# A two-layer spectral-convolution attention kernel: order of the work written out unit by unit, with five regroupings of its products

## The chip, the cores and the metric

The kernel runs on one core of one Trainium2 chip. The metric is the device time of one execution in microseconds (us); lower is better. Engines: PE (TensorE, matmuls), PEld (its weight loads), DVE (VectorE), ACT (ScalarE), POOL (GpSimd), SP (SyncE, which issues most transfers).

## The reference, cut to what matters

The input x has 2 batches of 56 planes of 128 x 128 points, all float32. Two layers of the same form follow each other, each `x = x + layer(gn(x))`:

```python
def layer(x, ...):                      # B, K, H, W = 2, 56, 128, 128; A = 8 heads
    xa = x.reshape(B * K, 1, H, W)
    xn = inorm(xa, g1, b1)
    k, q, v = (fno_layer(xn, ...) for each)          # 1 -> 8 channels
    scores = einsum('baks,bals->bakl', qh, kh) / sqrt(H * W)
    out = einsum('bakl,bals->baks', softmax(scores), vh)
    out = fno_layer(out, Pw, Pb, Psw, Psb)           # 8 -> 1 channel
    att = inorm(out + xa, gan, ban)
    an = inorm(att, g2, b2)
    h = fno_layer(an, M0..., norm=True, act=True)    # gelu
    h = fno_layer(h, M1..., norm=True)
    return inorm(h, gmo, bmo) + att

def fno_layer(x, w, b, sw, sb, norm=False, act=False):
    y = spectral_conv(x, w, b)          # rfft2, 2 x 16 x 16 modes times complex weights, irfft2
    if norm: y = inorm(y)
    y = y + skip1x1(x, sw, sb)
    return gelu(y) if act else y
```

`gn` normalises groups of 4 of the 128 positions of the last axis.

## The kernel before, in words

Everything is one function, `fno_layers` (L167). X2 holds x in SBUF, two halves of rows on partitions 0 to 55 and 64 to 119. P (8192 columns per batch) first holds the turned planes, later scratch and the gelu's output. WU, WT and WM hold block-diagonal mode weights; when these are done their room serves FB and `half`. Matmul results go to two PSUM pools: `bank` (2 buffers of one bank) and `pair` (3 buffers of two).

For each layer and each of the two batches the steps are:

- `turned` (L352) transposes X2 to planes by PE, ACT copies them to P, DVE takes `bn_stats` (L371).
- `modes_chain` (L457) gets mean and deviation, scales the planes (L479 on DVE, L477 on ACT, in four parts), transforms each part along one axis by PE (L483), turns it by DVE (L488), transforms along the other (`to_modes`, L384), and makes `gvr`, a row of 1/deviation for every position (L501).
- `gram` (L506, 128 products into one bank) and `gram_chain` give variances per plane.
- `scores` (L566): for each of four steps, 32 small products U x (L597, 64x64 weights from WU times 56 columns of modes) into a pair. The tile position is `(64 * e, 64 * e)`, so two of the array's four quarters are in use. ACT copies the pair (L602), and products with the modes add up the scores (L578).
- `scale_x` (L547) multiplies X2 by `gvr` on DVE, eight instructions a batch (L550), and sends the row to partitions 56 and 120.
- `values`, `softmax_chain`, `mix_chain`, `heads`, `norms_chain` (L611 to L746). `rows_of` (L427) makes diagonal matrices on DVE (L432) and `spread` (L435) turns them into rows on all partitions by one product with ones.
- `gelu` (L787): inverse transform by PE (`synthesis`, L753), skip product from X2 (`mixed`, L768), Gelu on ACT (L835), statistics (L837), turning back (L817), forward transform (L805).
- `h_chain` (L846): the modes of h, its weights, norms, `inverse`.
- `end` (L903): `synthesis` and `mixed` again, DVE adds the scaled h (L943). Then, in layer 0 and for batch 0 of layer 1, POOL adds the raw x (L946), which `moved` (L909) has loaded into one of three `xr` buffers, from the input x in layer 0 and from the DRAM buffer `store` in layer 1. In layer 0 the sum is the new X2, batch 0 is also written to `store`, and `turned` makes the next planes. For batch 1 of layer 1 (`last`), DVE divides X2 by the scale instead (L775) and PE adds it into the same pair (`add_x`, L782).

`prepare` (L237, on POOL) makes the mode weights of a layer compact; `relay` (L310) exchanges their axes in three groups, each one transpose, four DVE products with a mask and eight products on PE (L327); `build` (L334) and `build_m` spread them into WU, WT, WM on POOL (L337, L345).

The order of the work: every step is a generator that yields an estimated cost. `_woven` (L141) runs one step's units and fills each with units of another until the cost is reached; lines 961 to 1003 say which steps are woven. Instructions may then still be moved by the scheduler, which sorts each engine's instructions by priority and readiness; only those under `keep_in_program_order` stay put. A float32 matmul stands as two instructions in the trace, a transpose as one.

Of the kernel before, what the change touches and what calls it, by code (L numbers as in the profile page):

```python
# [57 lines left out]
def _constants():  # L58
# [26 lines left out]
    for r in range(2):  # L85
# [26 lines left out]
        "m16": (p[:, None] // 8 == np.arange(16)) * 1.0,  # L112
# [28 lines left out]
def _woven(lead, *bulks):  # L141

    rest = chain(*bulks)
    for want in lead:
        while want > 0:
            cost = next(rest, None)
            if cost is None:
                break
            yield cost
            want -= cost  # L150
    yield from rest


def _with(bulk, extra):

    for cost in bulk:
        next(extra, None)
        yield cost


def _run(units):
    for _ in units:
        pass
# [3 lines left out]
def fno_layers(ctx: ExitStack, tc: tile.TileContext, x, out, weights, small, const):  # L167
    nc = tc.nc
    V, S, G, T = nc.vector, nc.scalar, nc.gpsimd, nc.tensor
# [7 lines left out]
    dp = pool("dram", 1, space=bass.MemoryType.DRAM)  # L177
# [14 lines left out]


    Ct = cp.tile([N, N_CONST], F32, name="C")
    C = {k: Ct[:, o : o + n] for k, (o, n) in _PARTS.items()}
    ident = C["ident"]
    nc.scalar.dma_start(out=ident, in_=const["all"][:, :N])
# [4 lines left out]
    for b in range(B):  # L202
        for g in range(0, 8, 2):
            for c in range(2):
                nc.sync.dma_start(
# [3 lines left out]
            if (b, g) == (0, 4):  # L209
                nc.sync.dma_start(out=Ct[:, N:], in_=const["all"][:, N:N_CONST])  # L210
        if b == 0:
            for n in range(2):
                nc.sync.dma_start(out=smt[n], in_=small[n : n + 1, :].to_broadcast([N, N_SMALL]))
            nc.sync.dma_start(out=stage[:, :1088], in_=weights[0].rearrange("p m r n t -> p (m r n t)"))
    for b in range(B):
        nc.sync.dma_start(out=X2[K:64, b], in_=x[b, :8, :64, :])
    eps = cp.tile([N, 1], F32, name="eps")
    V.memset(eps, EPS)
    ones = cp.tile([N, N], F32, name="ones")
# [14 lines left out]
    store = dp.tile([1, K, N, N], F32, name="store")  # L234


    def prepare(layer):  # L237
        sml = smt[layer]
# [31 lines left out]
        tt(col("m2"), par["m1sw"], par["m1sw"], ALU.add)  # L270
        tt(Wf, Wf, _bc(rawc[:, 0], 1, 2 * N_W), ALU.mult)
        tt(M, M, _bc(rawc[:, 1:3], 2, N_W), ALU.mult)
        tt(W, W, M, ALU.add)
        tt(W[:, 0, 0:32, :], W[:, 0, 0:32, :], _bc(sml[:, 0:32], 2, 8), ALU.add)
        t64 = [stage[:, 544 + 64 * n : 608 + 64 * n].rearrange("p (a t) -> p a t", a=8) for n in range(4)]
# [29 lines left out]
        product(0, 1, 0, True, ss, g2, 3)  # L305
        product(16, 3, 2, False, vp, par["g1"], 5)
        place(cpt[:, 32:36].rearrange("p (n c) t -> p n c t", c=2), W[:, 0, 32:34, :], W[:, 1, 32:34, :], 5)
        return par, d, cpt, little(f"tc{layer}", [N, 8, 36])

    def relay(cpt, tcs, room, groups):  # L310

        L = room.rearrange("p (t e c j s) -> p t e c j s", t=8, e=2, c=2, j=4)
        for o, n in groups:
            rows = 8 * n
            pa = bank()
            T.transpose(pa[:rows, :N], cpt[:, o : o + n, :].rearrange("p n t -> p (n t)"), ident)
            src = pa[:rows, :N].rearrange("p (j c e t) -> p j c e t", j=4, c=2, e=2)
            for e in range(2):
                for c in range(2):
                    V.tensor_tensor(  # L320
# [363 lines left out]
    def heads(L, b, st):  # L684
# [3 lines left out]
        for t in range(8):  # L688
# [6 lines left out]
            if t % 2:  # L695
                yield 1.0
# [358 lines left out]
```

## Time and profile before

| what | us |
|---|---|
| median of 3 timed runs | 552.59 |
| the 3 runs | 560.3, 551.16, 552.59 |
| profiled execution, its own time | 547.76 |
| span of the profiled execution, first to last instruction | 546.0 |
| mean granted PE clock in it, as a share of full speed | 0.919 |

The profile is one execution. Busy times are of one engine each and overlap each other. A wait named in brackets is the idle time of an engine ahead of an instruction, with the one that ended it.

### The profile page before, as it was taken

The numbers are of one execution on the slowest core, as the hardware profiler recorded it, in microseconds if no ns is written. First come the engines' busy times: TensorE is split into PE (matmuls) and PEld (weight loads), VectorE is DVE, ScalarE is ACT, GpSimd is POOL, SyncE is SP. The second block draws the span as 40 slices with busy tenths as digits, with TensorE's granted clock in tenths as the row PEclk, the third lists the DMA queues.
The fourth block names the chain that finished last, engine by engine and source line by source line (L and its number), as shares of the span: only waits on it lengthen the run. The fifth ranks groups of instructions, "written<-read, shape, count | busy, mean of one in ns | idle before, by whom it ended". The sixth has DMA issues, their size and how long they took to land.

```text
span 546.0 us, 14842 instructions
## 1 busy us (share of the span) xinstructions
PE 458.8 (84%) x6696; PEld 315.0 (58%) x6696; DVE 318.6 (58%) x556; ACT 190.3 (35%) x242; POOL 158.5 (29%) x205
## 2 busy tenths in 40 slices
PE   2467999898699999989587799989599999986695
PEld 2325869686485566636443468778376556544431
DVE  1465352926735784777578562717715775766585
ACT  2443330524435436614223240344237356502000
POOL 2297509950000000044539924000000000055300
PEclk9998898989797998989679999999797998988698
DMA  8994001030100000016553320000000000027444
GB/s 181 232 196 73 4 2 46 4 89 2 20 2 2 1 2 1 1 35 212 175 136 100 98 78 6 3 4 4 2 3 1 1 2 1 1 56 236 149 129 141
DMA packets 13167, 33.24 MB, mean 61 GB/s; under 512 B 2080, under 2 KB 2848, under 8 KB 13088
## 3 DMA queue, kind: packets, MB, share of 16 engines
q1 hardware_dynamic: 12960, 32.23, 22.8%
q8 instruction: 52, 0.85, 0.7%
q10 hardware_dynamic: 144, 0.07, 0.1%
q14 instruction: 11, 0.09, 0.1%
HBM read 21.02 MB, written 11.01 MB: 59 GB/s over the span
## 4 chain that ended last, share of the span: by engine, by line
PE 53%; DVE 20%; POOL 7%; DMA 7%; ACT 6%; issue 5%; SPq 1%; DVEq 0%; POOLq 0%; ACTq 0%
PE pair L768 8%; PE pair L753 6%; PE pair L817 5%; POOL X L946 5%; PE pair L597 5%; PE bank L511 5%; PE bank L691 3%; DMA X<-x 3%; PE bank L805 3%; DMA xr<-x 3%; DVE WT L404 2%; DVE X L550 2%; PE bank L578 2%; PE bank L442 2%; PE bank L327 2%
## 5 line engine op out<-in xcount | busy, mean ns | idle before, releaser
L371 DVE BATCH_NORM_STATS2 stats<-P 128x6 f32<-128x448 f32 x64 | 36.1, 614 | 48.2 <-ACT P L366 32.3
L837 DVE BATCH_NORM_STATS2 stats<-P 128x6 f32<-128x512 f32 x64 | 40.7, 678 | 20.3 <-ACT P L835 20.3
L943 DVE SCALAR_TENSOR_TENSOR P<-P,hs,pair 128x1024 f32<-128x1024 f32 x32 | 40.1, 1270 | 12.7 <-PE pair L768 12.5
L835 ACT ACTIVATE P<-pair 128x1024 f32<-128x1024 f32 x32 | 32.6, 1025 | 32.4 <-PE pair L768 31.8
L946 POOL TENSOR_TENSOR X<-P,xr 128x1024 f32<-128x1024 f32 x16 | 37.5, 2355 | 19.4 <-DMA xr<-x 11.2
L393 POOL MEMSET WT<- 128x256 f32 x4 | 1.3, 313 | 139.4 <-PE bank L805 92.9
L817 PEld LDWEIGHTS pair<-C,P 120*128 120x128 f32 x256 | 29.0, 152 | 21.2 <-issue 8.5
L550 DVE TENSOR_TENSOR X<-X,gvr 120x1024 f32<-120x1024 f32 x32 | 40.3, 1303 | 0.0
L768 PE MATMUL pair<-X,Bs 57*64 57x512 f32 x256 | 40.2, 671 | 0.0
L768 PE MATMUL pair<-X,Be 57*64 57x512 f32 x256 | 38.6, 705 | 0.0
L817 PE MATMUL pair<-C,P 120*128 120x120 f32 x256 | 36.8, 291 | 0.5 <-DVE P L404 0.5
L511 PE MATMUL bank<-P 128*64 128x56 f32 (+1 forms) x1024 | 37.2, 238 | 0.0
L511 PEld LDWEIGHTS bank<-P 128*64 128x64 f32 (+1 forms) x1024 | 35.5, 152 | 2.1 <-issue 1.5
L597 PEld LDWEIGHTS pair<-xf,WU 64*64 64x64 f32 x1024 | 32.8, 135 | 5.3 <-issue 4.5
L597 PE MATMUL pair<-xf,WU 64*64 64x56 f32 x1024 | 35.9, 221 | 0.0
L818 ACT COPY WT<-pair 128x896 f32<-128x896 f32 x32 | 28.9, 906 | 14.0 <-PE pair L817 12.5
L753 PE MATMUL pair<-C,WT 32*128 32x128 f32 x512 | 24.1, 294 | 9.1 <-DVE WT L404 4.4
L753 PEld LDWEIGHTS pair<-C,WT 32*128 32x128 f32 x512 | 19.4, 189 | 20.5 <-issue 12.0
L369 ACT COPY P<-pair 128x896 f32<-128x896 f32 x16 | 14.5, 907 | 46.3 <-PE pair L363 46.3
L361 PE MATMUL pair<-C,X 56*128 56x56 f32 x256 | 16.7, 282 | 16.4 <-DMA X<-x 10.7
L363 PE MATMUL pair<-C,X 120*128 120x120 f32 x128 | 18.8, 297 | 13.4 <-POOL X L946 13.4
L363 PEld LDWEIGHTS pair<-C,X 120*128 120x128 f32 x128 | 14.9, 155 | 23.3 <-POOL X L946 20.0
(235 smaller groups left out, 850.0 us busy)
## 6 DMA issues: line engine op xcount, KB each, us to landing
X<-x SPq DMA_DIRECT2D x16, 448.0 KB
xr<-x SPq DMA_DIRECT2D x32, 224.0 KB
out<-P SPq DMA_DIRECT2D x32, 224.0 KB
store<-X SPq DMA_DIRECT2D x16, 224.0 KB
xr<-store SPq DMA_DIRECT2D x16, 224.0 KB
stage<-weights SPq DMA_DIRECT2D x2, 544.0 KB
C<-const_all SPq DMA_DIRECT2D x1, 621.0 KB
X<-x SPq DMA_DIRECT2D x2, 256.0 KB
```

The source lines that it names most:

```text
L363: T.transpose(p[:, s, N * e : N * e + 120], X2[:120, b, i, :], ident[:120, :120])
L371: V.bn_stats(stats[:, 2 * g + s, :], dst[:, 448 * s : 448 * s + 448])
L511: T.matmul(p[u : u + m, :K], lhsT=P[b][:, K * i : K * i + m], rhs=plane[b][:, i, :], start=(i < 2), stop=(i == N - 1), tile_position=(0, u ...
L550: tc.keep_in_program_order(V.tensor_tensor(v, v, _bc(st["gvr"][:120], 1, 8), ALU.mult))
L597: T.matmul(p[64 * e : 64 * e + 64, k, K * a : K * a + K], lhsT=WUv[64 * e : 64 * e + 64, t + k, a, :], rhs=xv[64 * e : 64 * e + 64, t + k, ...
L753: T.matmul(both[j // 2][:, j % 2, N * e : N * e + N], lhsT=Z[32 * j : 32 * j + 32, o : o + N], rhs=C["gw"][32 * j : 32 * j + 32, :], start ...
L768: T.matmul(p[64 * c : 64 * c + 64, r, :], lhsT=Bs[q, :], rhs=X2[q, b, s : s + 4, :].rearrange("p e w -> p (e w)"), start=False, stop=stop, ...
L817: T.transpose(p[:, r, N * e : N * e + 120], h3[:120, o : o + N], ident[:120, :120])
L835: S.activation(h3, both[v].rearrange("p r m -> p (r m)"), AF.Gelu)
L837: V.bn_stats(stats[:, 4 * A + 2 * v + r, :], h3[:, 512 * r : 512 * r + 512])
L943: V.scalar_tensor_tensor(h3, h3, st["hs"], both[v].rearrange("p r m -> p (r m)"), ALU.mult, ALU.add)
L946: G.tensor_tensor(dst, h3, xr[:, n % 3, :], ALU.add)
```

## The change

- **Order.** `_woven`, `_with`, `_run` and the costs go. Each step is a stream of units named by a letter and 2 x layer + batch; `ORDER` lists 714 units, and each entry runs the stream to its next `yield`. At the end `_in_order` ties every instruction of DVE, ACT, POOL, PE and SP to the one before it on its engine, so that no scheduler moves them.
- **U x** is a stream of its own (`u_x`), its tile position runs through all four quarters, and the scores take one copy of the modes with its halves exchanged (`xs`, two ACT copies).
- **Factor rows.** `rows` multiplies a broadcast column with diagonal matrices that `diagonals` (POOL) made once a layer.
- **Relay.** One group: POOL (in layer 0 POOL and DVE) masks the compact weights, and eight products of 288 columns add up in one bank.
- **Norm scale in the transform.** The scale is multiplied into the transform's 32 columns (`fwg`), the shift is added to the modes; `normalise` scales the planes for the Gram product apart from that. Two parts share one DVE turn.
- `scale_x` moves from DVE to POOL. In layer 1 both batches divide X2 by the scale, on POOL into `xr` (`end_x`), and PE adds it; `store` and its transfers go. The constants of both layers come in one transfer.

```diff
+ORDER = """
+t0 t0 t0 t0 t0 W0 t0 k0 k0 k0 k0 k0 t0 t0 k0 k0 k0 m0 m0 m0 W0 m0 m0 n0 n0 n0 t1 t1 t1 t1 m0 k1 k1 k1 t1 t1 m0 m0 W0
+W0 t1 t1 W0 R0 R0 n0 n0 n0 R0 R0 R0 B0 k1 k1 g0 g0 k1 k1 g0 g0 g0 k1 g0 m1 B0 m1 g0 g0 A0 c0 m1 m1 C0 n1 n1 u0 u0 m1
...
+y1 h0 y1 y1 z1 z1 z1 b1 b1 h0 h0 f1 f1 b1 b1 f1 h0 f1 f1 f1 b1 h0 h0 b1 f1 h0 f1 f1 h1 h1 e0 e0 o0 e0 e0 o0 h1 h1 x0
+x0 x0 e0 o0 x0 e0 o0 x0 t2 k2 A1 h1 h1 e0 h1 e0 o0 e0 o0 h1 h1 x0 e0 e0 o0 x1 t2 h1 e0 o0 h1 h1 h1 k2 t2 k2 A1 A1 A1
+t2 t2 k2 x1 k2 e1 e1 e1 x1 t2 t2 o1 o1 t2 x1 e1 e1 e1 k2 k2 o1 o1 e1 k2 e1 e1 x1 o1 x1 m2 x1 x1 e1 o1 e1 o1 e1 m2 t3
...
+e3 x3 e3 e3 o3 e3 x3 o3 o3 o3 e3 o3
+"""
...
+def _in_order(tc, engines):
+
+    last = {}
+    for i in list(tc.nc.cur_bb.bb.instructions):
+        if i.engine in engines:
+            if i.engine in last:
+                info = mybir.DependencyInfo(mybir.DependencyClass.NoSync, mybir.DependencyReason.DATA)
+                tc.add_manual_dep(i, last[i.engine], info, reason="in order")
+            last[i.engine] = i.name
...
-                nc.sync.dma_start(out=Ct[:, N:], in_=const["all"][:, N:N_CONST])
+                Q.dma_start(out=Ct[:, N:], in_=const["all"][:, N:])
...
+    def relay(layer):
...
+            E.tensor_tensor(
+                r.rearrange("p (s t n) -> p s t n", s=n, t=8),
+                _bc(cpt[:, :, s0 : s0 + n].rearrange("p n s -> p s n"), 2, 8), _bc(_bc(C["m8"], 1, n), 3, 36), ALU.mult,
+            )
...
+                T.matmul(
+                    p[:, :288], lhsT=C["sel"][:, 7 - s : 7 - s + N], rhs=r[:, 288 * (s - s0) : 288 * (s - s0) + 288],
+                    start=(s == 0), stop=(s == 7), skip_group_check=True,
+                )
...
+    def rows(cols, of):
+
+        p = bank()
+        for n, (u, m) in enumerate(zip(cols, of)):
+            T.matmul(p[:, K * n : K * n + K], lhsT=u.to_broadcast([K, N]), rhs=m, start=True, stop=True)
...
+        fwg = little(f"fwg{b}", [N, 32])
+        S.activation(fwg, C["fw"], AF.Copy, scale=gv)
...
+        p = to_modes(mid, by_h[L][0])
+        V.tensor_tensor(grid(xf[:, :448]), grid(p), _bc(sx, 2, K), ALU.add)
...
-            tc.keep_in_program_order(V.tensor_tensor(v, v, _bc(st["gvr"][:120], 1, 8), ALU.mult))
+            G.tensor_tensor(v, v, _bc(gvr[:120], 1, 8), ALU.mult)
...
+    def u_x(L, b):
+
+        R = room(b)
+        xv = grid(st[L][b]["xf"][:, :448])
+        for t in range(0, 8, 2):
+            p = pair()
+            for k in range(2):
+                for a in range(4):
+                    for c in range(2):
+                        for e in range(2):
+                            o, n = 64 * (e ^ c), 224 * k + K * a
+                            T.matmul(
+                                p[o : o + 64, c, n : n + K], lhsT=WUv[64 * e : 64 * e + 64, t + k, 4 * c + a, :],
+                                rhs=xv[64 * e : 64 * e + 64, t + k, :], start=True, stop=True,
+                                tile_position=(64 * e, o), skip_group_check=True,
+                            )
...
+    def end_x(L, b):
...
+                G.tensor_tensor(
+                    xr[:120, n % 3, :].rearrange("p (c s w) -> p c s w", c=2, s=4),
+                    x8.rearrange("p (c v s) w -> p v c s w", c=2, v=2)[:, n % 2], _bc(_bc(inv[:120], 1, 4), 1, 2), ALU.mult,
+                )
...
+    for name in ORDER.split():
+        _step(tc, name, streams[name])
+    assert all(next(s, "end") == "end" for s in streams.values())
+    _in_order(tc, [e.engine for e in (V, S, G, T, Q)])
```

The letters of the order: t transposes, k their statistics, m modes, n scaling of the planes, g Gram product, c its chain, q scale of X, u U x, s scores, v values, a softmax and mix, d heads, p norms, y gelu, z its statistics, b turning back, f forward transform, h the h chain, x load or division of X, e sums of the end, o its output; W `prepare`, R relay, O diagonals, A, B, C the builds of WU, WT, WM.

## Rows read from the trace of the kernel before

**Rows 1.** The page: busy us, share and instructions; chain that ended last.
```profile
PE 458.8 (84%) x6696; PEld 315.0 (58%) x6696; DVE 318.6 (58%) x556; ACT 190.3 (35%) x242; POOL 158.5 (29%) x205
...
PE 53%; DVE 20%; POOL 7%; DMA 7%; ACT 6%; issue 5%; SPq 1%; DVEq 0%; POOLq 0%; ACTq 0%
```

**Rows 2.** Windows: stretch, length, busy us per engine, clock, DMA share, GB/s.
```profile
0.00:52.00 52.00, 26.75 (x287) 17.89 (x289) 22.75 (x49) 18.97 (x22) 27.78 (x84) 1.00 0.83 179
52.00:232.00 180.00, 167.25 (x2655) 125.95 (x2659) 102.96 (x202) 73.04 (x95) 45.92 (x65) 0.92 0.06 13
232.00:331.00 99.00, 79.77 (x1005) 47.81 (x1006) 66.26 (x100) 28.72 (x35) 55.52 (x35) 0.90 0.41 115
331.00:480.00 149.00, 138.30 (x2252) 100.50 (x2252) 84.25 (x161) 65.72 (x83) 10.48 (x13) 0.94 0.03 3
480.00:546.00 66.00, 46.77 (x512) 22.81 (x512) 42.37 (x48) 3.89 (x8) 18.76 (x8) 0.85 0.48 147
...
500.00:520.00 20.00, 11.26 (x86) 6.22 (x84) 12.16 (x22) 1.00 (x4) 7.88 (x4) 0.66 0.54 164
```

**Rows 3.** Timeline of PE, five bursts: start us, length us, line, operation, tiles, count.
```profile
345.04 2.08 PE L597 MATMUL pair<-xf,WU 64*64 64x56 f32 x64
...
393.17 1.09 PE L620 MATMUL pair<-WT,xf 64*64 64x256 f32 x16
...
78.87 1.96 PE L327 MATMUL bank<-C,stage 128*128 128x16 f32 x16
...
519.47 1.09 PE L782 MATMUL pair<-X,C 56*64 56x512 f32 x8
...
246.44 1.04 PE L363 MATMUL pair<-C,X 120*128 120x120 f32 x8
```

**Rows 4.** Groups by line and shape: count, busy us, mean ns, idle before.
```profile
L550 DVE TENSOR_TENSOR X<-X,gvr 120x1024 f32<-120x1024 f32 x32 | 40.3, 1303 | 0.0
...
L946 POOL TENSOR_TENSOR X<-P,xr 128x1024 f32<-128x1024 f32 x16 | 37.5, 2355 | 19.4 <-DMA xr<-x 11.2 <-DVE P L943 8.1
...
L337 POOL TENSOR_TENSOR WU<-tc,C 128x1024 f32<-128x1024 f32 x8 | 16.3, 2055 | 2.5 <-ACT tc L331 2.5
...
L479 DVE TENSOR_SCALAR P<-P,gv,sh 128x1792 f32<-128x1792 f32 x8 | 10.2, 1281 | 0.3
...
L775 DVE TENSOR_TENSOR X<-X,gvr 120x1024 f32<-120x1024 f32 x8 | 9.5, 1223 | 6.9 <-PE pair L768 6.9
...
L432 DVE TENSOR_SCALAR dg<-C,k,der 56x56 f32<-56x56 f32 x8 | 2.1, 299 | 0.1
```

**Rows 5.** Timeline of layer 1's middle; in brackets idle time and who ended it.
```profile
377.47 3.48 DVE L550 TENSOR_TENSOR X<-X,gvr 120x1024 f32<-120x1024 f32 x3
...
389.39 0.86 PE L652 MATMUL bank<-C,P 56*64 56x56 f32 x10 [5.28 <-DVE Bs L450]
```

**Rows 6.** The chain that ended last, in order of time: start us, us, what.
```profile
251.99 2.34 POOL X L946
255.92 4.32 DMA xr<-x
...
538.81 1.28 DVE P L943
```

**Rows 7.** Timeline of POOL while layer 1's weights are prepared.
```profile
91.78 1.33 POOL L271 TENSOR_TENSOR stage<-stage,C 128x544 f32<-128x544 f32 x1
...
101.37 0.31 POOL L294 TENSOR_TENSOR stage<-stage 128x64 f32<-128x64 f32 x1
101.65 1.29 POOL L298 TENSOR_TENSOR stage<-stage 128x64 f32<-128x64 f32 x1
...
111.78 0.44 POOL L302 TENSOR_SCALAR stage<-stage,sm 128x64 f32<-128x64 f32 x1
```

**Rows 8.** The page's DMA issues: count and KB each.
```profile
store<-X SPq DMA_DIRECT2D x16, 224.0 KB
xr<-store SPq DMA_DIRECT2D x16, 224.0 KB
```

More of the change, by code (lines that the diff above doesn't have):

```diff
@@ L233, in fno_layers, with padded @@
     G.memset(xr.rearrange("p a b -> p (a b)"), 0.0)
-    store = dp.tile([1, K, N, N], F32, name="store")
+    def padded(name, rows, m, n):
+        both = [cp.tile([rows, n], F32, name=f"{name}{b}") for b in range(B)]
+        for t in both:
+            G.memset(t[:, m:], 0.0)
+        return both
+    xf_, gc_, BT_, Bs_, Be_ = (
+        padded(*a) for a in (("xf", N, 448, 456), ("gc", K, K, 64), ("BT", K, K, 64), ("Bs", N, K, 64), ("Be", N, K, 64))
+    )
+    over_all = cp.tile([K, 5 * K + N], F32, name="over")
+    over = over_all[:, : 5 * K].rearrange("p (n k) -> p n k", n=5)
+    over_dup = over_all[:, 5 * K :]
+    prs, tcs = [None, None], [None, None]
+    st = [[{}, {}], [{}, {}]]
     def prepare(layer):
+        if layer:
+            Q.dma_start(out=stage[:, :1088], in_=weights[1].rearrange("p m r n t -> p (m r n t)"))
         sml = smt[layer]
@@ L379, in to_modes, with count @@
+    def count(L, b):
+        stats = st[L][b]["planes"] = little(f"stats{b}", [N, 16, 6])
+        for n in range(16):
+            V.bn_stats(stats[:, n, :], P[b][:, 448 * n : 448 * n + 448])
+            if n % 2:
+                yield
     def to_modes(mid, over_h):
@@ L407, in inverse @@
             )
+            yield
     def multiply(n, src):
@@ L613, in values @@
+            yield
+        for c in range(2):
+            T.matmul(
+                sc[64 * c : 64 * c + 64, :224].rearrange("p (a l) -> p a l", a=4), lhsT=s["gc"],
+                rhs=SG[:K, 4 * c : 4 * c + 4, :], start=False, stop=True, tile_position=(0, 64 * c), skip_group_check=True,
+            )
+        yield
+    def values(L, b):
+        R, xf = room(b), st[L][b]["xf"]
         xv = grid(xf[:, :448])
@@ L814, in turn_back @@
+    def turn_back(L, b):
+        for n in range(8):
+            p = pair()
             for r in range(2):
@@ L894, in h_chain @@
+        yield
+        pads(half[b])
+        yield from inverse(L, grid(s1), half[b])
         p = bank()
[L895 to L923 removed]
@@ new lines, in end_sums @@
+                mixed(L, b, A, v, both[v], Be_[b], L == 0)
+                if L == 1:
+                    for c in range(2):
+                        for r in range(2):
+                            q = slice(64 * r, 64 * r + K)
+                            T.matmul(
+                                both[v][64 * c : 64 * c + 64, r, :], lhsT=C["fold"][q, :],
+                                rhs=xr[q, n % 3, 512 * c : 512 * c + 512], start=False, stop=True,
+                                tile_position=(64 * r, 64 * c), skip_group_check=True,
+                            )
@@ new lines, in fno_layers @@
+    streams = {}
+    for L in range(2):
+        streams[f"W{L}"] = prepare(L)
+        streams[f"R{L}"] = relay(L)
+        streams[f"O{L}"] = diagonals(L)
+        streams[f"A{L}"] = build(WUv, L, 0)
+        streams[f"B{L}"] = build(WTv, L, 16)
+        streams[f"C{L}"] = build_m(L)
+        for b in range(B):
+            for name, stream in (
+                ("t", turn), ("k", count), ("m", modes_chain), ("n", normalise), ("g", gram), ("c", gram_chain),
+                ("q", scale_x), ("u", u_x), ("s", scores), ("v", values), ("a", softmax_chain), ("d", heads),
+                ("p", norms_chain), ("y", gelu), ("z", gelu_stats), ("b", turn_back), ("f", forward), ("h", h_chain),
+                ("x", end_x), ("e", end_sums), ("o", end_out),
+            ):
+                streams[f"{name}{2 * L + b}"] = stream(L, b)
```

739 lines of the change are left out of this document (324 added, 415 removed).

## The prediction, made before the changed kernel was run

> **What bounds the kernel now.** I read the page's first and fourth parts, then the busy time of each engine in five stages, then groups of instructions by line, then the chain and the timeline where a stage loses time. The span is 546.0 us and TensorE (PE) is busy for 458.8 of it, DVE for 318.6, POOL for 158.5; on the chain that ended last PE has 53%, DVE 20%, POOL 7%, DMA 7% [rows 1]. So PE is the engine to count, and the question of each stage is how much of it is PE work at the full clock and how much is waiting or half clock.
>
> The stages [rows 2]: start (0 to 52 us: x arrives, 179 GB/s, until the first Gram product runs), the middle of layer 0 (52 to 232), the turn between the layers (232 to 331: both `end`s of layer 0, transposes, statistics, first Gram product of layer 1), the middle of layer 1 (331 to 480), and the end (480 to 546). The granted clock is one of two levels, 1.2 or 2.4 GHz, so a mean of 0.92 over 180 us says that 2 x 0.08 x 180 = 28.8 us went by at half; at full clock that work wants 14.4 us less (an upper value, since some of the half clock fell into idle time). PE work at full clock is then: layer 0 middle 167.25 - 14.4 = 152.9 of 180; turn 79.77 - 9.9 = 69.9 of 99; layer 1 middle 138.3 - 8.9 = 129.4 of 149; end 46.77 - 5 (half of 9.9, the stage idles much) = 41.8 of 66. Lost are 27, 29, 20 and 24 us.
>
> Where the losses sit. In both middles the 32 scalings of X by DVE (1.30 us each [rows 4]) stand in DVE's queue among the softmax and norm chains: three of them take 3.48 us at 377 us, and soon after PE is without work for 5.28 us until a DVE product lands [rows 5]; layer 0 has the same picture. All 32 come to 40.3 us of DVE [rows 4]. In the turn the chain runs alternately through POOL's add (2.35 us) and the reload of x (4.3 us) [rows 6]: for each of the 8 pieces two transfers bring x in while two of the same size take the new X out to `store` [rows 8]. At the end PE is busy for 11.26 of 20 us from 500 on [rows 2]: the last h chain runs when batch 0 has nothing left for PE, and behind PE's last work stand 7.2 us (538.8 to 546.0) of one DVE instruction and the last transfers [rows 6].
>
> **The change, part by part.**
>
> *U x in four quarters.* The 1024 matmuls stay; the stage's 64x64 products now cycle through four quarters of the array and no longer two. Before, 64 run in 2.08 us, 32.5 ns each [rows 3], 33.3 us for all. Upper gain: the values product uses four quarters already and passes 16 matmuls of 256 columns in 1.09 us [rows 3], which is 68 ns, or 1.06 ns a column in each quarter; at that rate 56 columns want 15 ns, and 17 us are saved. Lower gain: nothing, since no burst of the trace paces matmuls under 31 ns. Both rows are near, one in tiling and one in size; I take the middle, 8 us, four in each layer.
> The Trainium skill (TensorE: Matmul & The Clock Gate, What's actually happening) states a floor of about 25 ns from one matmul's start to the next, however small. No row here shows it. By that floor the saving would be 1024 x (32.5 - 25) = 7.7 us, and the sum the same.
>
> *Scale of X to POOL, and the layer-1 ends.* DVE loses 40.3 us (L550) and 9.5 us (L775) [rows 4]. POOL gains 32 products for `scale_x` and 16 for `end_x`, and loses the 8 layer-1 adds (8 x 2.36 = 18.9 us). A POOL product of 1024 columns costs 2.05 us (builds) to 2.36 us (adds) [rows 4]; I take the add, so +75.4 and +37.7 us. With the masks (below) POOL comes to about 158.5 - 18.9 + 113.1 + 7 = 260 us, a little over half of the new span. What covers it: the scaled X is wanted only by the first `mixed` after the norms, and PE has a whole attention stage before. Uncovered, one batch's scaling costs 8 x 2.36 = 18.9 us. A side gain: small POOL products of 64 columns take 0.31 us, but 1.29 us under DVE's scaling [rows 7]; that collision goes with L550.
> PE gains the added fold for batch 0 of layer 1: 64 matmuls, 8 in 1.09 us [rows 3], +8.7 us on the path at the end. The store to DRAM (16 transfers) and its reload (16) fall away [rows 8], which leaves half of the traffic in the turn.
>
> *Relay in one product.* Three groups of a transpose and 16 matmuls (1.96 us [rows 3]) per layer, at least 5.9 us of PE with DVE products between, become 16 matmuls of 288 columns. At the pace of the turn's transposes (8 of 120 columns in 1.04 us [rows 3], 1.08 ns a column) that is 0.31 us each, 5.0 us, so at least -0.9; at the 1.0 ns a column of the fold (512 columns in four quarters, 8 in 1.09 us) and with the transposes and the waits for DVE gone, at most -3. I take -2 us in each layer. POOL takes the masking, 1152 + 2304 columns, some 7 us at the builds' rate, off the path in layer 1. In layer 0 it is ahead of the WU build, so the start keeps its length.
>
> *Norm scale in the transform, factor rows by PE.* The first transform no longer waits for the scaled planes; that takes a first step of 1.3 us [rows 4] out of each of four chains, at most 5 us, and PE has other work in all but two of them (start, turn): -2. The diagonals (3 + 2 DVE steps of 0.3 us [rows 4], four times) leave the chains, and as many small matmuls come; between 0 and -5, I take -2. Both are within the losses counted below, not beside them.
>
> *One constants transfer.* 274 KB more come before the last quarter of batch 0: at 179 GB/s 1.5 us later. With the transform's gain the start stays at 52.
>
> *The order.* Every engine and the SP queue now run a written order. It costs nothing by itself; a wrong place makes PE wait with everything behind it. It lets the ends of layer 0 start inside the h chain, transposes of batch 0 run between batch 1's ends, and the last h chain run beside batch 0's ends.
>
> **The sum.** Start 52 (bounds 49 to 56). Layer 0 middle: 152.9 - 4 - 2 = 147 of work, and 7 of the 27 lost stay, since the scalings leave DVE's queue and the clock follows the gaps: 154 (147 to 174). Turn: PE work 69.9; POOL has 16 x 2.36 + 4 x 2.05 = 46 us and DVE 66 us [rows 2, 4], so nothing bounds above PE, but POOL's queue begins only after the first end: 74 (70 to 99). Layer 1 middle: 129.4 - 4 = 125, and 5 of 20 stay: 130 (121 to 145). End: 41.8 + 8.7 + 7.2 = 57.7, and 2 to 3 lost: 60 (57 to 70). Together 470. Around the span stand 1.8 us (547.76 against 546.0), so 471.8 against the profiled 547.76; the timed runs are 3.4 to 12.5 us above that one (551.16 to 560.3, median 552.59), of which I take the lowest: **475 us**.
>
> **The rivals.**
> 1. *Denser than that.* U x really doubles and no loss is left in the middles: 52 + 143 + 70 + 121 + 57 = 443, reported 448. For it: both middles are mostly PE already. Against it: softmax and norm chains are still there, and PE holds to its order.
> 2. *Half of the gain.* The written order meets late inputs in the turn and in layer 0 (POOL's adds behind WU builds, the relay ahead of the Gram product on PE): 52 + 165 + 85 + 140 + 64 = 506, reported 511. For it: PE can no longer pass a late unit. Against it: what is late can be summed from rows, 46 us of POOL beside 70 us of PE.
> 3. *POOL becomes the bound.* Place: the first `mixed` of each gelu, and the folds of the end. The builds, the second `prepare` and the masks stand in POOL's queue ahead of the scaling, so the scaled X comes late in all four batches: 4 x 18.9, and 37.7 at the end, 475 + 113 = 588. It decides the sign from 89 of these 113 us on (552.59 x 1.02 = 563.6). For it: POOL's work grows by some 100 us and its queue is first come, first served. Against it: before the first gelu of layer 0 POOL has 8 builds (16 us), the second `prepare` (20 us with the collisions, 91.8 to 112.2 [rows 7]), one batch's scaling (19) and some 10 us of smaller products, 65 in all, in the 100 us after the weights land. With half of it uncovered, 532 to 560, the time would be close to the old one.
> 4. *Four quarters do nothing:* the pace stays at 32.5 ns; the time is 483, inside the forecast's own range.
>
> **How the numbers follow.** Forecast with its own range 455 to 495: 0.56 (rival 4 in it). Rival 1: 0.16. Rival 2: 0.16. POOL half uncovered, no change that can be told: 0.06. Rival 3: 0.06. Two per cent, 11 us, is about what a measurement of this kernel can tell. Faster is the forecast with rivals 1, 2 and 4, 0.88; same 0.06; slower 0.06. The range goes down to rival 1 and up past rival 2: 445 to 520.
>
> **What would show it.** Right: POOL near 260 us and DVE near 260 us busy (318.6 less 49.8 of scaling, 6 of diagonals and the relay's products); PE near 430; the granted clock over 0.95 in both middles; no store in the DMA list; the first Gram product at about 52 us, layer 1's first at about 270, end after 60 us more from the last h chain. U x: 64 matmuls in 1.5 us (1.0 for rival 1, 2.08 for rival 4). Wrong: a wait of PE for a POOL product of X ahead of a gelu or a fold of more than 5 us (rival 3); a turn of over 85 us with PE waiting for POOL's adds or builds (rival 2); a start of over 56 us, with PE waiting for the masks.

## The result, and the profile after

The changed kernel takes 460.06 us (median of 4 runs, 459.57 to 462.2) beside 553.63 us for the kernel before on the same chip: ratio 0.833, 95% interval 0.8283 to 0.8376. The ratio is that of the fast runs alone and leaves out the one slow run, of 560.3 us, of the kernel before. The forecast was 475 us, with a range of 445 to 520.

The page of the changed kernel, its first and fourth parts [rows 1 before]:

```profile
span 457.4 us, 14855 instructions
PE 404.3 (88%) x6724; PEld 285.7 (62%) x6724; DVE 264.5 (58%) x457; ACT 186.8 (41%) x250; POOL 251.6 (55%) x263
...
PE 67%; DVE 14%; DMA 5%; POOL 5%; ACT 5%; issue 3%; SPq 0%; ACTq 0%; DVEq 0%; POOLq 0%
```

PE has 67% of the chain that ended last, before 53%; DVE went from 20% to 14%. POOL is busy 93 us longer, DVE 54 us less, and neither has more than 58% of the span.

The same five stages [rows 2], and 10 us of the last one; the columns are stretch, length, busy us (instructions) of PE, PEld, DVE, ACT and POOL, granted clock, DMA share, GB/s:

```profile
0.00:54.00 54.00, 28.22 (x318) 19.24 (x318) 28.80 (x46) 21.11 (x23) 28.06 (x73) 0.97 0.90 197
54.00:200.00 146.00, 139.69 (x2593) 107.22 (x2595) 72.52 (x144) 70.05 (x96) 86.59 (x106) 0.95 0.04 9
200.00:265.00 65.00, 60.91 (x877) 40.43 (x872) 59.17 (x88) 20.72 (x27) 49.77 (x26) 0.97 0.34 94
265.00:388.00 123.00, 119.06 (x2250) 87.68 (x2252) 61.58 (x120) 68.69 (x89) 56.69 (x45) 0.97 0.03 4
388.00:457.00 69.00, 56.42 (x704) 31.11 (x700) 42.46 (x62) 6.28 (x15) 30.49 (x14) 0.88 0.36 108
400.00:410.00 10.00, 5.85 (x35) 5.25 (x35) 6.66 (x24) 2.56 (x7) 0.00 (x0) 0.50 0.00 0
```

| stage | before | predicted | after |
|---|---|---|---|
| start, to the first Gram product | 52 | 52 | 54 |
| middle of layer 0 | 180 | 154 | 146 |
| turn | 99 | 74 | 65 |
| middle of layer 1 | 149 | 130 | 123 |
| end | 66 | 60 | 69 |

The marks at 54 and 200 us lie at the same products as those at 52 and 232 before; the marks at 265 and 388 do not lie at the products of 331 and 480. Between products of PE that both kernels have (start of each, us) the stretches are:

| up to | at, before | at, after | us before | us after |
|---|---|---|---|---|
| the first Gram product of layer 0 | 51.91 | 54.26 | 51.9 | 54.3 |
| the first synthesis of layer 0's ends | 233.68 | 199.57 | 181.8 | 145.3 |
| the first Gram product of layer 1 | 313.46 | 258.22 | 79.8 | 58.7 |
| the first synthesis of layer 1's ends | 477.85 | 412.38 | 164.4 | 154.2 |
| the last instruction | 546.0 | 457.4 | 68.2 | 45.0 |

The middle of layer 0 is 34 to 36 us shorter by either marks, the turn 21 to 34, and the start is no shorter. How much of the rest belongs to layer 1's middle (26 or 10 us) and how much to the end (nothing or 23) depends on the marks, because both h chains of layer 1 now stand, but for their last steps, ahead of its ends (388 to 412 us), where before one of them stood among the ends. In 400 to 410 us the two last h chains run side by side, PE has 5.85 us of work and runs at the lower of its two clocks.

Groups of instructions by line and shape, the first two of POOL and the others of PE (busy us, mean ns of one, idle before):

```profile
L609 POOL TENSOR_TENSOR X<-X,gvr 120x1024 f32<-120x1024 f32 x32 | 74.6, 2351 | 5.1 <-ACT gvr L561 5.1
L969 POOL TENSOR_TENSOR xr<-X,gvr 120x1024 f32<-120x1024 f32 x16 | 37.3, 2360 | 31.2 <-PE pair L989 31.2
...
L636 PE MATMUL pair<-xf,WU 64*64 64x56 f32 x1024 | 18.3, 220 | 1.4 <-issue 1.4
L831 PE MATMUL pair<-X,Bs 57*64 57x512 f32 x256 | 35.0, 663 | 0.0
L569 PE MATMUL bank<-P 128*64 128x56 f32 x1008 | 31.3, 223 | 0.5 <-DVE own L534 0.3 <-ACT P L548 0.2
```

The same three groups of PE in the kernel before:

```profile
L768 PE MATMUL pair<-X,Bs 57*64 57x512 f32 x256 | 40.2, 671 | 0.0
L511 PE MATMUL bank<-P 128*64 128x56 f32 x1008 | 36.8, 238 | 0.0
L597 PE MATMUL pair<-xf,WU 64*64 64x56 f32 x1024 | 35.9, 221 | 0.0
```

U x lost half of its busy time (35.9 to 18.3). But groups that the change does not touch shrank too: the skip product from 40.2 to 35.0 and the Gram product from 36.8 to 31.3, with as many instructions, while the mean of one fell by 1 and 6% only. A group's busy time is what its instructions cover together, so they now stand closer, and less of the time is at the lower clock (mean 0.952, before 0.919).

PE's timeline: the bursts that answer to [rows 3] (start us, us, line, tiles, count; idle time before in brackets):

```profile
48.27 3.90 PE L376 MATMUL bank<-WU,C 128*128 128x288 f32 x8 [1.66 <-POOL WU L369]
...
52.23 2.11 PE L376 MATMUL bank<-WU,C 128*128 128x288 f32 x8
...
54.26 1.96 PE L569 MATMUL bank<-P 128*64 128x56 f32 x59
...
64.19 1.16 PE L636 MATMUL pair<-xf,WU 64*64 64x56 f32 x64
```

64 products of U x take 1.16 us, 18 ns each, before 2.08. The relay's second eight take 0.26 us each; its first eight take 0.49, at a granted clock of 0.59 (48 to 52.2 us), so mostly at the lower level. What PE waits for in the whole span (us in total, times, longest):

```profile
PE pair L412 <- DMA X<-x: 12.7, 8, 2.8
PE pair L412 <- DMA C<-const_all: 5.7, 1, 5.7
PE bank L500 <- DVE mv L497: 3.3, 1, 3.3
```

No wait for POOL's scaling, adds or divisions stands in the whole list (the only one for POOL, 1.7 us, is for the relay's mask); the largest waits are the start's transfers. In the list of transfers `store` is gone, as written:

```profile
xr<-x SPq DMA_DIRECT2D x32, 224.0 KB
```

### The profile page after: what moved, and what is told of

Its sections match the earlier page's. It is cut to its first block, busy times and chain, and to the rows that moved or that the text cites. A ratio compares the mean times of both kernels' runs of the same rounds, so it can differ in the third digit from the quotient of the medians.

```text
span 457.4 us, 14855 instructions
## 1 busy us (share of the span) xinstructions
PE 404.3 (88%) x6724; PEld 285.7 (62%) x6724; DVE 264.5 (58%) x457; ACT 186.8 (41%) x250; POOL 251.6 (55%) x263
## 4 chain that ended last, share of the span: by engine, by line
PE 67%; DVE 14%; DMA 5%; POOL 5%; ACT 5%; issue 3%; SPq 0%; ACTq 0%; DVEq 0%; POOLq 0%
PE pair L831 11%; PE pair L816 8%; PE bank L569 7%; PE pair L863 6%; DMA sm<-small 4%; DVE P L1000 3%; PE pair L752 3%; PE pair L989 3%; PE pair L685 3%; PE pair L636 3%; PE bank L881 3%; PE bank L487 3%; PE bank L663 2%; PE pair L452 2%; PE bank L376 2%
## 5 line engine op out<-in xcount | busy, mean ns | idle before, releaser
L609 POOL TENSOR_TENSOR X<-X,gvr 120x1024 f32<-120x1024 f32 x32 | 74.6, 2351 | 5.1 <-ACT gvr L561 5.1
L969 POOL TENSOR_TENSOR xr<-X,gvr 120x1024 f32<-120x1024 f32 x16 | 37.3, 2360 | 31.2 <-PE pair L989 31.2
L1000 DVE SCALAR_TENSOR_TENSOR P<-P,hs,pair 128x1024 f32<-128x1024 f32 x32 | 40.4, 1275 | 18.7 <-PE pair L989 16.9
L425 DVE BATCH_NORM_STATS2 stats<-P 128x6 f32<-128x448 f32 x64 | 34.7, 612 | 18.3 <-ACT P L417 18.3
L831 PE MATMUL pair<-X,Bs 57*64 57x512 f32 x256 | 35.0, 663 | 0.0
L831 PE MATMUL pair<-X,Be 57*64 57x512 f32 x256 | 33.8, 617 | 0.0
L569 PE MATMUL bank<-P 128*64 128x56 f32 (+1 forms) x1024 | 31.7, 222 | 0.5 <-DVE own L534 0.3
L863 PE MATMUL pair<-C,P 120*128 120x120 f32 x256 | 31.1, 271 | 0.8 <-ACT P L847 0.7
L412 PEld LDWEIGHTS pair<-C,X 56*128 56x128 f32 x256 | 12.6, 178 | 23.3 <-DMA X<-x 10.6
L387 POOL TENSOR_TENSOR WT<-tc,C 128x1024 f32<-128x1024 f32 x8 | 15.5, 1952 | 16.0 <-PE bank L435 11.9
L816 PE MATMUL pair<-C,P 32*128 32x128 f32 x512 | 22.1, 302 | 0.1
L816 PEld LDWEIGHTS pair<-C,P 32*128 32x128 f32 x512 | 18.8, 201 | 3.4 <-issue 2.5
```

What stands on the lines that cost most here:

```text
L425: V.bn_stats(stats[:, n, :], P[b][:, 448 * n : 448 * n + 448])
L569: T.matmul(p[u : u + m, :K], lhsT=P[b][:, K * i : K * i + m], rhs=plane[b][:, i, :], start=(i < 2), stop=(i == N - 1), tile_position=(0, u ...
L609: G.tensor_tensor(v, v, _bc(gvr[:120], 1, 8), ALU.mult)
L816: T.matmul(both[j // 2][:, j % 2, N * e : N * e + N], lhsT=Z[32 * j : 32 * j + 32, o : o + N], rhs=C["gw"][32 * j : 32 * j + 32, :], start ...
L831: T.matmul(p[64 * c : 64 * c + 64, r, :], lhsT=Bs[q, :], rhs=X2[q, b, s : s + 4, :].rearrange("p e w -> p (e w)"), start=False, stop=stop, ...
L863: T.transpose(p[:, r, N * e : N * e + 120], h3(b, n)[:120, o : o + N], ident[:120, :120])
```

## The experiments

Two questions: which part of the change brings the 92 us, and whether the reason given for the vanished waits (the scaling leaves DVE's queue, the store transfers go) holds. The prediction gives the order no price of its own and lays the vanished waits to the regroupings; the rival is that the order and the tie bring it. All ratios are to the kernel before.

### The order and the tie

The changed kernel without the tie:

```diff
-    _in_order(tc, [e.engine for e in (V, S, G, T, Q)])
```

> The changed kernel without the tie of each engine's instructions to the written order: the same program order, but the scheduler may move instructions. Theory (the list of units is what counts, the tie only keeps it): within 2%, 452 to 470. Rival (the scheduler breaks the list up): 475 to 500.

505.83 us (504.18 to 506.44), ratio 0.915 (0.91 to 0.92): 46 us slower than tied. Its waits of PE, and what POOL did then:

```profile
PE bank L376 <- POOL WU L369: 11.5, 1, 11.5
```

```profile
31.87 0.93 POOL L652 TENSOR_TENSOR P<-C,der 56x448 f32<-56x448 f32 x1
...
35.45 1.36 POOL L311 TENSOR_TENSOR stage<-stage,C 128x544 f32<-128x544 f32 x1
...
54.06 4.69 POOL L369 TENSOR_TENSOR WU<-stage,C 128x1152 f32<-128x1152 f32 x1
```

The scheduler fills POOL with factors for the scores (L652, in the tied kernel at 73.61 us) and other small steps that are wanted much later. Compacting the weights (L311) so begins at 35.45 us, tied at 27.04; the relay's mask (L369) runs at 54.06 and not at 45.47, PE stands for 11.5 us, and its first Gram product comes at 67.73 us and not at 54.26. Small ready steps pass the one that the chain waits for: this is what the tie excludes. Of the 44 us between the two spans 13 are lost here; the other 31 lie between this Gram product and layer 1's ends, and what caused them stays open.

Next, the changed kernel with the kernel before's sequence: `ORDER` holds the units as the old weave ran them, without the tie. In the first of two such lists the planes were scaled before the transform read them, so the modes that it computes differ from the reference's; the second list has that in place.

```diff
 ORDER = """
-t0 t0 t0 t0 t0 W0 t0 k0 k0 ...
+(the units in the sequence of the old weave)
 """
...
-    _in_order(tc, [e.engine for e in (V, S, G, T, Q)])
```

> The changed kernel with a list of units that repeats the weave of the kernel before, and not tied: the regroupings without the new order. Theory (regroupings and order each give about half of the 93 us): 500 to 515. Rival A (regroupings carry it, PE work down by 54 us): 470 to 480. Rival B (order carries it): 530 or more.

561.08 us (558.83 to 562.96), ratio 1.0153 (1.0092 to 1.0214).

> The changed kernel with the weave of the kernel before as its list of units, the scheduler free to move instructions: the regroupings alone. In a first run of such a list 561 us were measured. Theory (the regroupings by themselves give nothing, the order is everything): 545 to 565. Rival (regroupings give half): under 520.

557.14 us (554.9 to 561.17), ratio 1.0105 (1.0022 to 1.0189). All regroupings together, in this list of the old sequence, give nothing. Its busy times and three waits of PE:

```profile
PE 442.0 (79%) x6724; PEld 292.0 (52%) x6724; DVE 261.5 (47%) x457; ACT 194.2 (35%) x254; POOL 252.5 (45%) x263
```

```profile
PE pair L413 <- POOL X L1001: 20.8, 3, 17.8
PE pair L411 <- DVE WT L524: 19.1, 1, 19.1
PE pair L451 <- DVE P L797: 14.2, 1, 14.2
```

DVE and POOL are as busy as after (264.5 and 251.6), PE less than before (458.8), and yet the span is 559.4: what was saved in work went into single waits of PE of 14 to 19 us. What stood ahead of each:

```profile
52.47 2.22 DVE L368 TENSOR_TENSOR WU<-stage,C 128x1152 f32<-128x1152 f32 x1 [20.13 <-POOL stage L330]
...
151.87 0.21 DVE L796 TENSOR_TENSOR pair<-P,bank 1x56 f32<-1x56 f32 x1 [14.55 <-POOL P L774]
...
316.57 16.15 POOL L608 TENSOR_TENSOR X<-X,gvr 120x1024 f32<-120x1024 f32 x7
...
332.66 2.35 POOL L1001 TENSOR_TENSOR X<-P,xr 128x1024 f32<-128x1024 f32 x1
```

All three come from POOL's queue. DVE's half of the relay's mask (L368) waits 20 us for POOL's preparing of the weights, with the transform's turn (L524) behind it; a copy of one row (L774) stands on POOL behind the preparing of layer 1's weights; and seven scalings, 16 us, run ahead of the add (L1001) that PE's transposes want. The first Gram product comes at 75.31 us, 23 us later than before, but from there to layer 0's ends (244.81) it is 169.5 us and not 181.8. So gains and losses cancel in this list; that the regroupings give nothing in any list of the old kind is not shown. The same list with the tie:

```diff
+    _in_order(tc, [e.engine for e in (V, S, G, T, Q)])
```

> The same old weave, with each engine tied to it. Theory A (the tie by itself is worth what it is worth under the new list, 45 us): about 515. Theory B (the old list was made for a scheduler that repairs it; tied, PE waits in every chain): 560 or more.

571.98 us (570.09 to 574.2), ratio 1.0368 (1.0299 to 1.0436). The three long waits are gone here (the longest for POOL is 6.3 us), but shorter ones take their place: PE is busy for 447.4 of 570.3 us. All four cells have the regroupings in them:

| us | sequence of the old weave | sequence of the change |
|---|---|---|
| free for the scheduler | 557.14 | 505.83 |
| tied | 571.98 | 460.06 |

The list is worth 51 us untied and 112 tied; the tie is worth 46 us with the new list and costs 15 with the old one. So the rival stands: the tie is no gain by itself, it makes the sequence count, good or bad. What the new list is worth without the regroupings is not known: neither that nor the kernel before with its own sequence tied was tried.

### The regroupings, alone in the kernel before

The scaling of X on POOL, nothing else:

```diff
-            tc.keep_in_program_order(V.tensor_tensor(v, v, _bc(st["gvr"][:120], 1, 8), ALU.mult))
+            tc.keep_in_program_order(G.tensor_tensor(v, v, _bc(st["gvr"][:120], 1, 8), ALU.mult))
```

> The kernel before with one part of the change: the scaling of X on POOL and not on DVE, nothing else. Theory (the prediction's step: the scalings in DVE's queue held the softmax and norm chains): 10 to 15 us less, 538 to 545. Rival (without the new order the regroupings are worth nothing, as the old weave showed): 549 to 560.

561.74 us (560.58 to 563.59), ratio 1.0241 (1.0131 to 1.0351): slower, by 1.3 to 3.5%. The timeline of the place of [rows 5], now without DVE's scaling (of POOL's seven scalings on end, the last five):

```profile
380.00 11.55 POOL L550 TENSOR_TENSOR X<-X,gvr 120x1024 f32<-120x1024 f32 x5
...
381.84 9.97 DVE L432 TENSOR_SCALAR dg<-C,k,der 56x56 f32<-56x56 f32 x2
...
392.08 0.93 PE L437 MATMUL bank<-dg,ones 56*128 56x168 f32 x2 [6.48 <-DVE dg L432]
...
402.95 0.85 PE L652 MATMUL bank<-C,P 56*64 56x56 f32 x10 [5.29 <-DVE Bs L450]
```

and DVE's group of the diagonals in that run:

```profile
L432 DVE TENSOR_SCALAR dg<-C,k,der 56x56 f32<-56x56 f32 x8 | 22.6, 2862 | 0.1
```

Two things are to be seen. The wait of 5.28 us that the prediction laid to the scalings in DVE's queue is still there, 5.29 us: it belongs to the softmax chain, a row of short steps from L638 on, and to the norm steps behind it up to L450, and no scaling stands between them. In both runs of the old list with all regroupings, PE has no wait at this product (L716 there), before 13.2 us over the four batches (10.6 for L450, 2.6 for L645). So these waits can go without the new order, by a regrouping other than the scaling or by the way the old weave is written there as units; which it was is open. And a new wait came: two diagonals, 0.52 us before, take 9.97 us beside POOL's scalings and end at 391.81 us, just behind the last of these (391.55); all eight went from 2.1 us [rows 4] to 22.6. The collision of [rows 7] has turned round: DVE is now the one that stands.

The Trainium skill (SBUF — State Buffer, "SBUF: two separate sides") says that a DVE instruction in a two-port mode or with two SBUF inputs, and a GpSimd one, exclude each other on a shared port pair: the one that starts first has it for its whole instruction. The trace agrees that these diagonals and the scalings exclude each other (whether the diagonals ran in such a mode it does not show); but with POOL's 2.3 us for one, two waits of one instruction would be 4.7 us, and 9.97 were measured.

In the changed kernel the diagonals are POOL's and the rows come from PE, so that nothing of the kind stands beside the scaling. Its timeline where six scalings run in one piece:

```profile
288.98 13.97 POOL L609 TENSOR_TENSOR X<-X,gvr 120x1024 f32<-120x1024 f32 x6
...
296.49 0.39 DVE L710 TENSOR_TENSOR P<-bank,tot 128x224 f32<-128x224 f32 x1
```

DVE's softmax steps beside it take their usual 0.4 us; they read `bank`, which is in PSUM. A reciprocal on SBUF among them (L709, 0.18 us at 296.27) is not stopped either. So the factor rows, valued at 2 us in the sum, also keep the scaling on POOL from stopping DVE; that is read from these rows, not tried by itself.

Next, the layer-1 ends by division and PE, without `store`:

```diff
-        last = L == 1 and b == 1
+        last = L == 1
...
-                if L == 1 or b == 0:
+                if L == 1:
```

> The kernel before with one part of the change: batch 0 of layer 1 takes its x back from X2 as batch 1 does (DVE divides, PE adds), so the store to DRAM and its reload go. Theory (the turn was bound by these transfers): the turn falls from 99 to 85 us and the end grows by up to 9 us of folds and 9.5 us of DVE: 540 to 550. Rival (POOL's adds bound the turn, the transfers hide): 555 to 565.

560.93 us (555.52 to 564.91), ratio 1.0133 (1.0021 to 1.0246). The turn of that kernel, the columns as in the windows above:

```profile
232.00:331.00 99.00, 82.77 (x1016) 50.16 (x1016) 65.43 (x99) 28.75 (x38) 56.44 (x36) 0.88 0.25 64
```

The transfers of the turn fell from 115 to 64 GB/s, and at 331 us the same Gram product of layer 1 begins (331.07; in the kernel before 332.78, 1.7 us later). The store transfers did not hold the turn. The end grew from 66 to 73.7 us (480 to 553.7), near the 8.7 us of PE that the prediction gave to the added fold.

### The regroupings, undone in the changed kernel

The scaling on DVE, in both layers:

```diff
-            G.tensor_tensor(v, v, _bc(gvr[:120], 1, 8), ALU.mult)
+            V.tensor_tensor(v, v, _bc(gvr[:120], 1, 8), ALU.mult)
```

> The changed kernel with the scaling of X back on DVE, at the same places of the order. Theory (DVE's queue was what held the softmax and norm chains): 32 x 1.3 us stand in front of them again, 8 to 20 us more, 468 to 480, with POOL at 177 us busy and DVE at 305. Rival (POOL at 55% is now in the way of builds and adds): no change or a faster kernel, 450 to 460.

493.82 us (492.21 to 497.49), ratio 0.8947 (0.8885 to 0.9009): 34 us slower. Up to the first Gram product of layer 1 (257.98 us, in the changed kernel 258.22) nothing is lost. All of it is lost in the middle of layer 1, which takes 156 us and not 123:

```profile
265.00:421.00 156.00, 128.40 (x2242) 94.31 (x2236) 84.83 (x136) 68.99 (x89) 22.14 (x28) 0.87 0.02 3
```

```profile
336.58 2.38 DVE L609 TENSOR_TENSOR X<-X,gvr 120x1024 f32<-120x1024 f32 x2
...
342.86 4.05 PE L831 MATMUL pair<-X,Bs 57*64 57x512 f32 x16 [5.82 <-DMA X<-gvr]
...
358.18 10.17 DVE L609 TENSOR_TENSOR X<-X,gvr 120x1024 f32<-120x1024 f32 x4
...
359.77 6.36 POOL L969 TENSOR_TENSOR xr<-X,gvr 120x1024 f32<-120x1024 f32 x2
...
371.02 0.26 DVE L800 TENSOR_SCALAR dcq<-pair,der 1x56 f32<-1x56 f32 x1
...
371.34 3.46 PE L863 MATMUL pair<-C,P 120*128 120x120 f32 x16 [9.47 <-DVE dcq L800]
...
393.45 4.18 PE L831 MATMUL pair<-X,Bs 57*64 57x512 f32 x16 [6.44 <-DMA X<-gvr]
```

Three waits of PE come to 21.7 us: two ahead of a skip product, for the scaled X and its row (5.82 and 6.44), and one behind four scalings that stand in DVE's queue ahead of a step of 0.26 us (9.47). The mean granted clock of the stage is 0.87, in the changed kernel 0.97. The four scalings take 10.17 us, where one alone takes 1.2: POOL's divisions (L969), which only layer 1 has, run beside them. If the place in the queue, or these divisions, are what costs, the same edit in layer 0 costs nothing:

```diff
-            G.tensor_tensor(v, v, _bc(gvr[:120], 1, 8), ALU.mult)
+            (V if L == 0 else G).tensor_tensor(v, v, _bc(gvr[:120], 1, 8), ALU.mult)
```

> The scaling of X runs on DVE in layer 0 alone; layer 1 keeps it on POOL. Theory (what the earlier run with all 32 scalings on DVE lost, it lost in the middle of layer 1, where two scalings stand in DVE's queue ahead of a product that TensorE waits for; in layer 0 the 16 scalings are covered): 460 us, within 4 us of the changed kernel, DVE about 286 us busy and POOL about 218, the first Gram product of layer 1 at 258 us as in both. Rival (DVE time on the norm and softmax chains costs wherever it stands, 34 us for 32 scalings): half of it, 475 to 479 us.

461.69 us (459.33 to 463.39), ratio 0.8326 (0.8265 to 0.8387), no difference from the changed kernel. Its middle of layer 0:

```profile
54.00:200.00 146.00, 138.63 (x2599) 104.90 (x2602) 91.82 (x162) 70.26 (x97) 54.47 (x90) 0.97 0.05 11
```

DVE has 91.82 us of work here and not 72.52, and the stage is as long. So it isn't DVE's load by itself that costs, but what stands at these places in layer 1: scalings ahead of wanted steps, and divisions beside scalings. The share of each stays open, and whether a list made for DVE's scaling would find other places for them wasn't tried.

U x, first in the loop order that keeps two quarters for eight products on end:

```diff
-                for a in range(4):
-                    for c in range(2):
+                for c in range(2):
+                    for a in range(4):
```

> The changed kernel with its U x products issued so that only two quarters of the array are in use at a time (the two loops over a and c exchanged; the same 1024 matmuls). In the changed kernel 64 of them run in 1.16 us, before in 2.08. Theory (PE bounds the kernel almost everywhere): the pace goes back to about 2.0 us for 64, 16 bursts, and all of the 14 us come back: 474. Rival (the saved time was only turned into waits for the scaled planes, the builds of WU and the ACT copies): under 5 us, 460 to 465.

460.78 us (460.18 to 464.27), ratio 0.8361 (0.8295 to 0.8426). The pace went less than half of the way back (before 2.08, after 1.16):

```profile
63.44 1.54 PE L636 MATMUL pair<-xf,WU 64*64 64x56 f32 x64
...
L636 PE MATMUL pair<-xf,WU 64*64 64x56 f32 x1024 | 23.0, 223 | 0.5 <-issue 0.5
```

5 us more of PE (23.0 against 18.3) and no change that can be told: as an undoing it failed, since the old pace didn't come back. So every product is issued twice instead:

```diff
-                for a in range(4):
+                for a in [0, 1, 2, 3] * 2:
```

> The changed kernel with every U x product issued twice into the same place (2048 matmuls and not 1024). At the changed kernel's pace (64 in 1.16 us) that is 18.6 us more PE work. Theory (PE time in this stage is on the path): 15 to 19 us more, 475 to 479. Rival (the stage has slack, which the run with two quarters hints at: its bursts took 1.5 us and its time did not move): under 6 us more, up to 466.

485.53 us (483.88 to 493.42), ratio 0.8789 (0.8719 to 0.886), 25 us slower:

```profile
L636 PE MATMUL pair<-xf,WU 64*64 64x56 f32 x2048 | 34.4, 219 | 7.9 <-issue 7.8
```

The second 1024 add 16.1 us of busy time and 6.5 us of idle time before them. So U x is on the path when it grows by that much; of the 5 us of the run before nothing showed. How much of the 17.6 us comes off the span stays open, between these two.

### A better order by hand

The end is the only long stage left with waits in it. The last 108 units were rearranged, so that the h chain of batch 0 runs among batch 1's gelu and batch 0's ends fill batch 1's h chain; in the same run the relay's masks of layer 0 are both DVE's.

```diff
-z3 y3 f3 b3 b3 z3 f3 b3 f3 f3 f3 f3 h3 h3 h3 h2 h2 h2 h3 z3 z3 h3 h3 h3 h2 h3 h3 h2 h3 h2 h2 x2 x2 h3 h2 e2 e2 e2 e2
-e2 x2 x2 x2 e2 o2 o2 o2 o2 h3 h3 e2 x2 e2 e2 x2 e2 e2 x3 e2 e3 e3 x3 x3 o2 x3 e3 x3 e3 e3 x3 o2 o2 o2 o3 o3 o3 e3 e3
...
+y3 h2 h2 z2 h2 f3 f3 f3 z3 y3 y3 h2 b3 b3 z3 h2 f3 f3 f3 y3 h2 y3 y3 z3 z3 h2 b3 b3 f3 f3 f3 z3 z3 x3 h2 h3 h3 h2
+h2 h3 h3 h3 h2 x2 x2 e2 e2 e2 x2 x2 o2 h3 o2 e2 h3 e2 h3 h3 e2 x2 x2 o2 o2 e2 e2 e2 x2 h3 o2 o2 e2 e2 e2 x3 x3 x3
...
-        room = [(0, 4, WU[:, :1152], G), (4, 4, WU[:, 1152:2304], V)] if layer == 0 else [
+        room = [(0, 4, WU[:, :1152], V), (4, 4, WU[:, 1152:2304], V)] if layer == 0 else [
```

> The changed kernel with another order of its last 108 units, and with the layer-0 relay masks both on DVE. The second h chain of layer 1 starts when batch 0's forward transforms are done, with batch 1's gelu between its steps, and the ends of batch 0 fill the other h chain. In the changed kernel PE stands at 5.85 of 10 us and half clock from 400 to 410, with both h chains side by side. Theory (the chain waits there are on the path): the first end's synthesis starts at about 400 and not 412, 10 to 14 us less in all, 444 to 450. Rival (the wait only moves into batch 1's gelu): 456 to 464. The relay: the DVE half took 4.47 us beside two POOL products; both halves on DVE should take 1.4 us each, the first Gram product at 51 to 52 and not 54.3.

476.89 us (467.52 to 482.98); no interval is given for it, and the shortest run is 7 us above the changed kernel. A second list, with the h chain of batch 0 still earlier:

```diff
-y3 h2 h2 z2 h2 f3 f3 f3 z3 y3 y3 h2 b3 b3 z3 h2 f3 f3 f3 y3 h2 y3 y3 z3 z3 h2 b3 b3 f3 f3 f3 z3 z3 x3 h2 h3 h3 h2
+h2 h2 z2 h2 y3 f3 f3 f3 h2 y3 h2 y3 b3 h2 h2 b3 z3 z3 f3 f3 f3 y3 y3 y3 h2 z3 z3 b3 b3 h2 h2 f3 f3 f3 h2 z3 z3 x3
...
```

> As the run before, with the first h chain's steps set closer together and less of batch 1's gelu between. Theory: within 3 us of that run, since PE has work between in either order. Rival (PE, held to its order, waits for each step of the chain): 5 to 10 us slower than that run.

479.45 us (474.63 to 482.29), ratio 0.8702 (0.8593 to 0.8811): 19 us slower than the changed kernel. The end of this run, and PE's wait for the sums of the end (L1000) in it:

```profile
388.00:476.70 88.70, 68.17 (x736) 34.77 (x736) 48.74 (x71) 11.54 (x19) 30.60 (x14) 0.86 0.27 84
```

```profile
PE pair L816 <- DVE P L1000: 5.0, 5, 1.8
```

The first `end` product comes at 405.44 us and not at 412.38, as meant, but then PE waits time and again for DVE's steps, 0.7 to 1.8 us each, and the granted clock is 0.77 to 0.86 in each 10 us from 420 to 460. In the changed kernel PE has no wait after the first `end` product, and the clock is 0.99 to 1.00 from 410 to 440. That reads as if the ends of one batch, spread between the chain's steps, were too thin to fill PE; it was not tried by itself. Nothing found here beats 460 us. The masks on DVE gained nothing either: DVE's mask beside POOL's takes 4.47 us in the changed kernel, and both on DVE take 4.45 us together in this one.

## Why the prediction was right, and where it was not

- **Sign and size.** Faster by 17%, 15 us under the forecast, inside its own range. By the marks of the windows the inner stages came out 8, 9 and 7 us shorter than predicted, the end 9 longer, the start 2 longer. Taken at the products nearest to the prediction's own marks (331 us is layer 1's second Gram product, 332.78 before and 277.33 after; 480 the first synthesis of its ends) the middle of layer 0 is 9 shorter, the turn 4 and the middle of layer 1 5 longer, and the end 15 shorter. Layer 1's first Gram product came at 258.22 us, "about 270" predicted, layer 0's at 54.26 ("about 52"). So the middle of layer 0 is well shown; that the other stages sum up near the forecast is in part luck.
- **U x** was the term mis-sized: "the middle, 8 us", measured 17.6 us (35.9 to 18.3), the upper bound drawn from the values product (17 in the text; its 1024 x 17.5 ns are 17.9). The floor of 25 ns that the Trainium skill states (TensorE: Matmul & The Clock Gate, "Wait — 56ns, not 53.3ns?", and not in the section that the prediction names) does not hold here: 18 ns.
- **PE's work.** The sum took PE's busy time, less half of the clock's loss, as a fixed amount of work. By the same reckoning the middle of layer 0 has 139.69 - 0.05 x 146 = 132 us of it where 147 were predicted, and 14 lost where 7 were. Busy time of untouched groups fell by 13 to 15%: it was no floor.
- **Half clock.** "Over 0.95 in both middles" was 0.95 and 0.97.
- **The reason for the vanished waits fell.** "The scalings leave DVE's queue" and the lighter traffic in the turn: alone they gave +2.4 and +1.3%, and the 5.28 us wait stayed. That wait is also gone with all regroupings in the old list, so it did not need the new order; but there waits of 14 to 19 us behind POOL's queue came for it, and none of those is in the changed kernel. The step on the order, "It costs nothing by itself; a wrong place makes PE wait", was half of it: the list and the tie together take 97 us from 557. The step that failed is this one: the vanished waits were given to two parts, and the order had no term of its own. The gain belongs to the parts and the order together: the parts in the old list gave nothing, and one part less in the new list (the scaling) costs 34 us.
- **POOL.** 251.6 us, predicted 260; the cover held, and no gelu or fold waited for a scaled X, so the rival with POOL as the bound fell for this list. In the old list its mechanism did come: PE waits 17.8 us for an add behind seven scalings. What the prediction missed is the other side of the collision: POOL's scaling stops DVE's diagonals, which cost 20 us of DVE more in the kernel before.
- **DVE** 264.5 us (predicted 260), **PE** 404.3 (430).
- **The turn**, whose chain was read as running "alternately through POOL's add (2.35 us) and the reload of x (4.3 us)": without the store it is 2 us shorter. In the new order its window of 65 us has 60.91 of PE.
- **The end** supposed the last h chain beside batch 0's ends. The written list has both h chains together ahead of nearly all ends, at half clock (5.85 of 10 us); from the last chain's first product (392.99) it is 64 us to the end, predicted 60. Two lists by hand with the chain nearer to what the prediction had thought were 7 us slower or more, and 19.
- **The relay** was 0.26 us a product against the 0.31 taken, but 0.49 in the first eight at half clock: near 0 in layer 0, where the start is 2 us longer.

## What to carry to other kernels

Regroupings that take work off the busy engines can be worth nothing (557 us) while the work that they move stands in another queue ahead of a short step that PE waits for; in a list made for them one alone (the scaling on POOL) is worth 34 us. A sequence and its tie should be tried together and apart: here the tie made the good list better and the poor one worse. That a long instruction stands ahead of a wait doesn't show that it causes it: take it away and see whether the wait goes. And a stage's length is compared between two kernels at the same instruction, not at a round time.

## What the runs showed of the hardware that was not expected

- Matmuls of 64x64 weights and 56 columns: 64 take 2.08 us with two quarters in use, 1.54 us with two quarters for eight on end and then the other two, 1.16 us with four in turn. The order of issue alone makes 0.38 us of it.
- DVE instructions on SBUF operands beside POOL's products can be stopped for longer than one POOL product: 9.97 us for two that take 0.52, and in another place 11.57; both times they end just behind the last of seven products that POOL runs on end (391.81 against 391.55 us, 132.04 against 131.79). The softmax steps that read `bank` in PSUM were not (0.38 us). POOL is stopped too: a copy of 128x128 took 2.21 us beside DVE's mask, and 0.29 us otherwise.
